# Counting edges in a graph layer: when the copies out of PSUM may start

## The chip, the cores and the metric

The kernel runs on one core of a Trainium2 chip. The metric is the device time of one execution in microseconds (us). The engines are TensorE (PE, with its weight loads shown apart as PEld), VectorE (DVE), ScalarE (ACT), GpSimd (POOL) and SyncE (SP). Each engine takes its instructions in the order in which the program lists them; what crosses from one engine to another is a wait on a semaphore.

## What is computed

Two message-passing layers on a graph of 12,500 nodes with 32 values each and 200,000 edges, sorted by destination. Cut to what matters:

```python
h = relu(layernorm(x))
# first layer: sum over edges, scaled by the degrees
hn  = h * rsqrt(max(out_deg, 1))
agg = segment_sum(hn[src], dst)
x   = x + (agg * rsqrt(max(in_deg, 1))) @ W + b
# second layer: a small network on every edge, then a mean
h   = relu(layernorm(x))
m   = mlp(concat(h[dst], h[src] - h[dst]))      # 64 -> 64 -> 128 -> 64 -> 32
x   = x + segment_sum(m, dst) / max(in_deg, 1)
```

## The kernel before

The kernel works through the edges in tiles of 128. It has three stages: out-degrees and the normalised node table (up to about 500 us of the profile), the sums of the first layer (to about 1930 us), and the second layer.

The first layer sums its messages in three ways side by side. Early chunks have their rows gathered before the degrees are known and are scaled later (`scale_rows`, tiles `look`, `mask`, `rows_scaled`). The next chunks gather rows of the finished table by indirect DMA on POOL (`gather_chunk`, `sum_rows`, PSUM tile `ps_late`). The last 491 tiles gather nothing: they are *counted* (`count_edges`), and the change is in these.

A counted tile works like this. The destinations of 128 sorted edges span at most 13 nodes (`WD`). A source node is a high part (one of 98, `PART`) and a low part (one of 128). For each edge DVE makes a one-hot row of the low part (`lo`, 128 wide) and a one-hot row of high part and destination together (`oh`, 98 x 13 wide, cut in three ranges of high parts, `THIRDS`: 33, 33 and 32 of them). The product of the two (L789) counts how many edges go from each source to each of the 13 destinations. The three ranges are 429, 429 and 416 columns; the first two go to the PSUM tile `count_two` (two banks), the third to `count_third` (one bank). ACT copies both out of PSUM into the tile `count` in SBUF (L791), as two copies of 858 and 416 columns. PSUM has one buffer of each of the two tiles, so the next tile's products wait for this tile's copies. PSUM is full: `count_two` 2 banks, `count_third`, `look`, `ps_late`, `st2`, `nu_ps` and `kept` one each.

Eight counted tiles make a group. When a group's counts are complete, `multiply` (L730) multiplies the node table with them: 98 products of 104 columns (L738, tile `st`), done in five portions of 19 or 20 during the first five tiles of the next group, then a copy (L745), a transposition (L752), another copy (L754), a placing product (L757) and an addition to the sums on DVE. In the order of PE's queue a portion stands before the tile's counts in tiles 0 to 4; the transposition and the placing product stand behind the counts of tiles 5 and 6 (`LATE`).

`count_edges` is a generator and takes one step per tile; the loop at L807 lets it run between the gathers, `sum_rows`, `scale_rows` and the node updates (`update_nodes`, tiles `nu_...`), so all of their products share PE's queue with the counts. The order is written out by hand (`manual_schedule`); the framework adds the waits.

The lines that the change touches, as they are before:

```python
ps = pp.tile([P, len(ranges), 512], F32, name=f"count_{name}")
...
    nc.tensor.matmul(
        ps[:, k, :w], lo[:, i % TPC // 2, :, i % 2], oh[:, k0 + k, :w, i % 2], start=True, stop=True)
nc.scalar.activation(
    counts[g][:, t, a:b, :].rearrange("p (k h) d -> p k (h d)", k=len(ranges)), ps[:, :, :w], AF.Copy)
```

Of the kernel before, what the change touches and what calls it, by code (L numbers as in the profile page):

```python
# [8 lines left out]
F32 = mybir.dt.float32  # L9
# [3 lines left out]
AF = mybir.ActivationFunctionType  # L13
# [3 lines left out]
P = 128  # L17
# [16 lines left out]
TPC = 4  # L34
# [50 lines left out]
def gnn_kernel(  # L85
# [20 lines left out]
    nc = tc.nc  # L106
# [133 lines left out]
    for at in pieces:  # L240
        h, a = hx[:, at, :D], xp[:, at, :]
# [44 lines left out]
    with tc.tile_pool(name="deg", bufs=3) as hp, tc.tile_pool(  # L286
        name="deg_ps", bufs=1, space=bass.MemoryType.PSUM
# [33 lines left out]
        def one_hots(name, k, width, b):  # L321

            hot = hp.tile([P, HG, width, HT], BF16, name=name)
            n = min(HG, (NT - b) // HT)
            nc.vector.tensor_tensor(  # L325
                hot[:, :n], hl[:, k, b : b + n * HT].rearrange("p (g t) -> p g t", t=HT)[:, :, None, :].to_broadcast(
                    [P, n, width, HT]), lane_g[:, None, :width, :].to_broadcast([P, n, width, HT]), op=OP.is_equal)
            return hot

        for b in batches:  # L330
            to = min(EARLY, RAW + -(-(EARLY - RAW) * (b // (HG * HT) + AHEAD_HG) // len(batches)))
            if to > gathered:
                c = slice(gathered * TPC, to * TPC)
# [5 lines left out]
            lo = one_hots("lo", 1, P, b)  # L339
            for t in range(b, min(NTR, b + HG * HT)):  # L340
                g, i = divmod(t - b, HT)
# [12 lines left out]
        for at in pieces:  # L354
            h = hx[:PART, at, :D]
# [3 lines left out]
            for k in range(3):  # L359
                t = terms[:, :, k * D : (k + 1) * D]  # L360
# [19 lines left out]
        for b in range(0, NT, P):  # L380
            n = min(P, NT - b)
# [51 lines left out]
    with tc.tile_pool(name="flag", bufs=1) as fp, tc.tile_pool(  # L433
        name="flag_ps", bufs=1, space=bass.MemoryType.PSUM
    ) as pp:
        lo = fp.tile([P, 1], F32, name="lo")
# [161 lines left out]
    with tc.tile_pool(name="e0", bufs=8) as sp, tc.tile_pool(name="nu", bufs=1) as np_, tc.tile_pool(  # L598
        name="direct", bufs=1) as dp, tc.tile_pool(name="e0_ps", bufs=1, space=bass.MemoryType.PSUM) as pp, tc.tile_pool(
        name="nu_ps", bufs=1, space=bass.MemoryType.PSUM) as np_ps:  # L600
# [113 lines left out]
        for a, b in THIRDS:  # L714
            nc.scalar.dma_start(
                table[:, a:b, :D3], tab_hn[OFF + P * a : OFF + P * b, :].rearrange("(h l) c -> l h c", l=P))
        los, onehots, counts = {}, {}, {}
        LATE = (TD - 3, TD - 2)

        def onehots_of(i):  # L720

            if i % TPC == 0:
                c = DIR * TPC + i
                los[i // TPC] = one_hots(dp, hl[:, 1, c : c + TPC], P, "lo", 3)
            onehots[i // 2] = oh = dp.tile([P, 3, KW, 2], BF16, name="oh", bufs=4)
            nc.vector.tensor_tensor(  # L726
                oh, keys[:, :, i : i + 2][:, :, None, :].to_broadcast([P, 3, KW, 2]),
                count_h[:, None, :, :].to_broadcast([P, 3, KW, 2]), op=OP.is_equal)

        def multiply(g):  # L730


            c, tiles = counts.pop(g), min(TD, ND - g * TD)
            ps = pp.tile([P, P + STEP], F32, name="st2")
            n = TD - 3
            for s in range(n):
                for h in range(PART * s // n, PART * (s + 1) // n):
                    nc.tensor.matmul(  # L738
                        ps[:, : tiles * WD], table[:, h, :], c[:, :tiles, h, :], start=(h == 0), stop=(h == PART - 1))
                if s < n - 1:  # L740
                    yield
            some = dp.tile([D3, WD * TD], F32, name="some")
            if tiles < TD:
                nc.vector.memset(some, 0.0)
            nc.scalar.activation(some[:, : tiles * WD], ps[:D3, : tiles * WD], AF.Copy)  # L745
            width = STEP * (GD - 1) + W
            place = dp.tile([WD * TD, width], F32, name="place")
            nc.vector.tensor_scalar(
                place, count_h[: WD * TD, :width, 0], pos[:, g : g + 1], None, op0=OP.is_equal)
            yield  # L750
            ps = pp.tile([P, P + STEP], F32, name="st2")
            nc.tensor.transpose(ps[: WD * TD, :D3], some, ident[:D3, :D3])  # L752
            turned = dp.tile([WD * TD, D3], F32, name="some_t")
            nc.scalar.activation(turned, ps[: WD * TD, :D3], AF.Copy)  # L754
            yield
            ps = pp.tile([P, P + STEP], F32, name="st2")
            nc.tensor.matmul(ps[:D3, :width], turned, place, start=True, stop=True)  # L757
            yield
            chunks = range(DIR + GD * g, min(NCH, DIR + GD * (g + 1)))
            sums.add(slice(0, D3), STEP * chunks[0], ps[:D3, : STEP * (len(chunks) - 1) + W], vector=True)  # L760
            added(chunks)
            yield

        def count_edges():


            before = iter(())
            onehots_of(0)
            onehots_of(2)
            for i in range(ND):  # L770
                g, t = divmod(i, TD)
                if t == 0:
                    for _ in before:
                        assert False
                    if g > 0:
                        before = multiply(g - 1)
                    counts[g] = dp.tile([P, TD, PART, WD], BF16, name="count", bufs=2)
                if i % 2 == 0 and i + 4 < ND:
                    onehots_of(i + 4)
                oh, lo = onehots[i // 2], los[i // TPC]  # L780
                if t not in LATE:
                    next(before, None)

                for ranges, name in ((THIRDS[:2], "two"), (THIRDS[2:], "third")):
                    k0, a, b = THIRDS.index(ranges[0]), ranges[0][0], ranges[-1][1]
                    ps = pp.tile([P, len(ranges), 512], F32, name=f"count_{name}")
                    w = (b - a) // len(ranges) * WD
                    for k in range(len(ranges)):
                        nc.tensor.matmul(  # L789
                            ps[:, k, :w], lo[:, i % TPC // 2, :, i % 2], oh[:, k0 + k, :w, i % 2], start=True, stop=True)  # L790
                    nc.scalar.activation(  # L791
                        counts[g][:, t, a:b, :].rearrange("p (k h) d -> p k (h d)", k=len(ranges)), ps[:, :, :w], AF.Copy)
                if t in LATE:
                    next(before, None)
                next(updating)
                yield i
            for rest in (before, multiply(NDG - 1)):
                for _ in rest:
                    next(updating)
                    yield ND  # L800

        counting = count_edges()
        LAG = 2

        QUICK = 5
        steps, stages = DIR - EARLY - 6, ND + 2 * TD
        for m in range(EARLY, DIR + LAG + 1):  # L807
# [10 lines left out]
            i = m - EARLY  # L818
# [24 lines left out]
    with tc.manual_schedule(), tc.tile_pool(name="prep", bufs=3) as prep, tc.tile_pool(name="e1", bufs=3) as ep, tc.tile_pool(name="fn", bufs=2) as fp, tc.tile_pool(  # L843
        name="p1_ps", bufs=2, space=bass.MemoryType.PSUM
# [158 lines left out]
    with tc.If(bad > 0):  # L1003
        sums0 = dram.tile([NROW, D + 1], F32, name="sums0")
        sums1 = dram.tile([NROW, D], F32, name="sums1")
        with tc.tile_pool(name="gp", bufs=1) as gp, tc.tile_pool(name="ge", bufs=1) as ge, tc.tile_pool(
            name="ge_ps", bufs=1, space=bass.MemoryType.PSUM
# [49 lines left out]
            with tc.For_i(0, NTR, 1) as i:  # L1057
                s, d, same, r = edges(i)
# [4 lines left out]
                ps = gps.tile([P, D3], F32, name="g_ps")  # L1063
# [8 lines left out]
            for q in range(NQ):  # L1072
                n = min(J, NBLK - J * q)
# [10 lines left out]
            with tc.For_i(0, NTR, 1) as i:  # L1084
                s, d, same, r = edges(i)
# [4 lines left out]
                a = ge.tile([P, HID], F32, name="g_a")  # L1090
# [17 lines left out]
                ps = gps.tile([P, D], F32, name="g_ps")  # L1108
# [7 lines left out]
            c = gp.tile([P, NBLK], F32, name="g_c")  # L1116
# [39 lines left out]
```

## Time and profile before

| What | us |
|---|---|
| Median of 3 runs (lowest, highest) | 4297.05 (4295.58, 4301.9) |
| The profiled execution, its own time | 4360.52 |
| Its span, first to last instruction | 4358.4 |
| Stretch of the first layer's sums in the profile | 498 to 1930 |
| Products of the first two ranges, L789, 982 of them | 320.5 busy |
| Copies of `count_two`, L791, 491 of them | 434.8 busy |
| Copies of `count_third`, L791, 491 of them | 252.1 busy |

How to read it: a row of the profile names the line of the kernel, the engine, the operation, what it writes and reads, shapes and number, then its busy time and the mean time of one, and last the idle time of the engine just ahead of it with what ended that idle time. In a list of waits, each row has the waiting engine and line, who ended the wait, and the sum in us, the number and the longest. In a timeline, each row has start and length in us and, in brackets, the idle time before it. The ends of products on PE are modelled, their starts are recorded. The mean granted clock of TensorE was 0.76 of full speed over the span.

### The profile page before, as it was taken

To read this page: it belongs to the slowest core of one execution; us is meant where nothing else is said; L and a number is where in the kernel's file an instruction comes from. 1 tells how busy PE (TensorE), PEld (TensorE's weight loads), DVE (VectorE), ACT (ScalarE), POOL (GpSimd) and SP (SyncE) were. 2 spreads that over 40 slices of the span, in tenths; PEclk is the share of its full clock that TensorE was granted. 3 is DMA by queue.
4 is the path that set the end of the run, shared out by engine and by line. 5 is a ranking of instruction groups with operands and counts; after the bars stand their busy time and mean duration, and the time that the engine had idled before them with its cause. 6 is when DMAs were issued, how large, how long until landed. Compare 5 with 4: busy or idle time off the path is not lost.

```text
span 4358.4 us, 54122 instructions
## 1 busy us (share of the span) xinstructions
PE 2926.1 (67%) x20860; PEld 1950.4 (45%) x20860; DVE 1822.0 (42%) x4113; ACT 1107.2 (25%) x2034; POOL 2495.7 (57%) x2655
## 2 busy tenths in 40 slices
PE   2444276777767777763667777777777777777777
PEld 2333154555555555551344444444444444444445
DVE  6555465656656566541223223222232232232233
ACT  0000254454544545430111111111111111111112
POOL 6555354545545555545566666666666666666663
PEclk9995588888888888875667777666777677677777
DMA  3110211111111111111222222222222222222221
GB/s 77 11 11 10 60 20 19 24 22 26 25 24 24 20 26 28 22 37 35 45 50 51 50 50 54 50 51 50 51 52 49 54 51 50 51 52 53 50 51 31
DMA packets 234664, 170.64 MB, mean 39 GB/s; under 512 B 156040, under 2 KB 182888, under 8 KB 234400
## 3 DMA queue, kind: packets, MB, share of 16 engines
q0 software_dynamic: 84320, 75.96, 11.6%
q1 hardware_dynamic: 131338, 85.26, 7.5%
q10 hardware_dynamic: 18742, 5.89, 0.7%
q8 instruction: 168, 2.75, 0.3%
q14 instruction: 96, 0.79, 0.1%
HBM read 153.98 MB, written 12.92 MB: 38 GB/s over the span
## 4 chain that ended last, share of the span: by engine, by line
PE 44%; another core or an unknown queue 18%; issue 14%; DVE 10%; ACT 8%; POOL 4%; DMA 1%; DVEq 0%; ACTq 0%; POOLq 0%
PE p L940 8%; ACT count L791 6%; PE p L930 6%; PE count_two L789 5%; PE st L738 5%; PE ps L958 4%; PE p L916 4%; POOL gj L211 4%; PE p L912 3%; DVE lo L325 2%; PE count_third L789 2%; PE ps_late L641 1%; DVE hi L325 1%; PE look L677 1%
## 5 line engine op out<-in xcount | busy, mean ns | idle before, releaser
L211 POOL DMA_INDIRECT gj<-tab_j,src_j x1563 | 1474.8, 944 | 912.8 <-issue 418.1
L211 POOL DMA_INDIRECT rows<-tab_hn,src_j x816 | 770.2, 944 | 755.3 <-PE ps_late L641 401.2
L940 PE MATMUL p<-w3s,h 128*128 128x64 f32 x3128 | 513.3, 322 | 158.8 <-issue 123.5
L791 ACT ACTIVATE count<-count_two 128x858 bf16<-128x858 f32 x491 | 434.8, 886 | 632.7 <-remote 270.6
L943 DVE TENSOR_TENSOR h<-p,b3n 128x512 f32<-128x512 f32 x196 | 135.2, 690 | 1052.2 <-remote 473.4
L940 PEld LDWEIGHTS p<-w3s,h 128*128 128x128 f32 x3128 | 472.3, 234 | 203.3 <-issue 159.1
L932 ACT ACTIVATE h<-p,b2s 128x1024 f32<-128x1024 f32 x196 | 217.8, 1111 | 1170.6 <-remote 453.6
L789 PE MATMUL count_two<-oh,lo 128*128 128x429 bf16 x982 | 320.5, 414 | 289.8 <-ACT count L791 219.0
L738 PE MATMUL st<-count,table 128*128 128x104 bf16 (+1 forms) x6076 | 423.2, 225 | 133.2 <-issue 82.2
L738 PEld LDWEIGHTS <-table 128*128 128x128 bf16 x6076 | 379.0, 104 | 198.1 <-issue 148.3
L930 PE MATMUL p<-h,w2s 64*128 64x512 f32 x782 | 393.2, 877 | 94.2 <-issue 80.1
L726 DVE TENSOR_TENSOR oh<-keys,kept 128x2574 bf16<-128x2574 f16 x246 | 365.5, 1487 | 60.6 <-remote 30.3
L958 PEld LDWEIGHTS ps<-hot,h 128*64 128x64 f32 x3126 | 238.2, 172 | 296.4 <-issue 174.1
L958 PE MATMUL ps<-hot,h 128*64 128x128 f32 x3126 | 272.9, 329 | 124.0 <-DVE h L943 122.3
L916 PE MATMUL p<-turned,ai 128*64 128x512 f32 x782 | 317.9, 843 | 26.7 <-issue 26.6
L789 PEld LDWEIGHTS <-lo 128*128 128x128 bf16 x1473 | 150.2, 109 | 413.6 <-issue 363.5
L342 PE MATMUL deg_ps<-hi,lo 128*128 128x98 bf16 x1563 | 183.1, 270 | 196.9 <-issue 138.3
L211 POOL DMA_INDIRECT rows_early<-tab_h,src_j x224 | 211.4, 944 | 158.0 <-DVE src_j L334 89.4
L560 DVE TENSOR_TENSOR acc<-acc,ps 64x64 f32<-64x64 f32 (+1 forms) x198 | 44.6, 225 | 594.8 <-remote 253.4
L912 PE MATMUL p<-ident,gj 128*128 128x128 f32 x784 | 199.0, 369 | 109.1 <-issue 108.5
L892 DVE TENSOR_TENSOR turned<-row,kept 128x512 f32<-128x512 f16 x391 | 249.7, 679 | 37.3 <-PE p L912 15.3
L791 ACT ACTIVATE count<-count_third 128x416 bf16<-128x416 f32 x491 | 252.1, 513 | 5.7 <-issue 1.9
(201 smaller groups left out, 2914.6 us busy)
## 6 DMA issues: line engine op xcount, KB each, us to landing
row<-rel_row SPq DMA_DIRECT2D x195, 256.0 KB
gj<-tab_j,src_j POOLq DMA_INDIRECT x1563
rows<-tab_hn,src_j POOLq DMA_INDIRECT x816
ai<-tab_i SPq DMA_DIRECT2D x195, 64.0 KB
srow<-hi_row SPq DMA_DIRECT2D x64, 98.0 KB
rows_early<-tab_h,src_j POOLq DMA_INDIRECT x224
tab_j<-nu_aij SPq DMA_DIRECT2D x23, 128.0 KB
tab_i<-nu_aij SPq DMA_DIRECT2D x23, 128.0 KB
```

The lines of the kernel that those rows point to most:

```text
L211: nc.gpsimd.indirect_dma_start(out=tile_ap, out_offset=None, in_=table, in_offset=bass.IndirectOffsetOnAxis(ap=col, axis=0))
L726: nc.vector.tensor_tensor(oh, keys[:, :, i : i + 2][:, :, None, :].to_broadcast([P, 3, KW, 2]), count_h[:, None, :, :].to_broadcast([P, 3, ...
L738: nc.tensor.matmul(ps[:, : tiles * WD], table[:, h, :], c[:, :tiles, h, :], start=(h == 0), stop=(h == PART - 1))
L789: nc.tensor.matmul(ps[:, k, :w], lo[:, i % TPC // 2, :, i % 2], oh[:, k0 + k, :w, i % 2], start=True, stop=True)
L791: nc.scalar.activation(counts[g][:, t, a:b, :].rearrange("p (k h) d -> p k (h d)", k=len(ranges)), ps[:, :, :w], AF.Copy)
L892: nc.vector.tensor_tensor(turned, v["row"][:, k], part_f.to_broadcast([P, CHUNK]), op=OP.is_equal)
L912: nc.tensor.matmul(p1[:, t, :], v["gj"][:, t].rearrange("p k c -> p (k c)"), ident, is_transpose=True, start=(t == 0), stop=False, skip_gr ...
L916: nc.tensor.matmul(p1[k * HID : (k + 1) * HID].rearrange("p t e -> p (t e)"), v["ai"][:, k], v["turned"][k], start=False, stop=True, skip_ ...
L930: nc.tensor.matmul(p2[:, k], w2s[s, :], v["h1"][s, :], start=True, stop=True)
L932: nc.scalar.activation(h2[:, :n], p2[:, :n], AF.Relu, bias=b2s)
L940: nc.tensor.matmul(p3[:, k * TPC + t, :], v["h2"][:, k, t * P : (t + 1) * P], w3s, start=True, stop=True)
L958: nc.tensor.matmul(ps[k * HID : (k + 1) * HID, o : o + W], v["h3"][:, k * TPC + t, :], v["hot"][k][:, t, :], start=(i == 0 and t == 0), st ...
```

## The change

There are three edits in `count_edges` and just above it.

First, `count_two` and `count_third` are two PSUM tiles made once, instead of being taken anew from the pool for each counted tile. Their size and number of buffers (one each) stay.

Second, the product of the third range is split in two: one of its first 8 columns and one of its other 408. Both load the same weights (`lo`). So there are four products for a tile instead of three, each with its weight load.

Third, both copies are written after all four products, and each is given a dependency on the last of them (`end`, the 408 columns). In the program that results, the copy of `count_two` waits for that product's signal instead of that of the second range, and the copy of `count_third` behind it on ACT's queue has no wait left to do. The wait of the third range for the copy of the tile before stands at the product of 8 columns. Everything else on the five engines keeps its order.

```diff
+        count_ps = {name: pp.tile([P, n, 512], F32, name=f"count_{name}") for name, n in (("two", 2), ("third", 1))}
         LATE = (TD - 3, TD - 2)
+        FIRST = 8
...
+                copies = []
                 for ranges, name in ((THIRDS[:2], "two"), (THIRDS[2:], "third")):
                     k0, a, b = THIRDS.index(ranges[0]), ranges[0][0], ranges[-1][1]
-                    ps = pp.tile([P, len(ranges), 512], F32, name=f"count_{name}")
+                    ps = count_ps[name]
                     w = (b - a) // len(ranges) * WD
                     for k in range(len(ranges)):
-                        nc.tensor.matmul(
-                            ps[:, k, :w], lo[:, i % TPC // 2, :, i % 2], oh[:, k0 + k, :w, i % 2], start=True, stop=True)
-                    nc.scalar.activation(
-                        counts[g][:, t, a:b, :].rearrange("p (k h) d -> p k (h d)", k=len(ranges)), ps[:, :, :w], AF.Copy)
+
+                        for c in (slice(0, w),) if name == "two" else (slice(0, FIRST), slice(FIRST, w)):
+                            end = nc.tensor.matmul(
+                                ps[:, k, c], lo[:, i % TPC // 2, :, i % 2], oh[:, k0 + k, c, i % 2], start=True, stop=True,
+                                skip_group_check=True)
+                    copies.append((counts[g][:, t, a:b, :].rearrange("p (k h) d -> p k (h d)", k=len(ranges)), ps[:, :, :w]))
+
+                for to, of in copies:
+                    tc.add_manual_dep(
+                        nc.scalar.activation(to, of, AF.Copy).ins, end.ins.name,
+                        mybir.DependencyInfo(mybir.DependencyClass.Sync, mybir.DependencyReason.DATA))
```

## The prediction

> **What bounds the kernel now.** I read the engines' busy time first, then the same by stretch of time, then the waits of the stretch that the change touches, then the timeline of single tiles.
>
> ```profile
> PE 2926.1 (67%) x20860; PEld 1950.4 (45%) x20860; DVE 1822.0 (42%) x4113; ACT 1107.2 (25%) x2034; POOL 2495.7 (57%) x2655
> ```
>
> No engine is full. By stretches (PE, weight loads, DVE, ACT, POOL busy us):
>
> ```profile
> 498.00:1930.00 1432.00, 1008.21 (x9940) 745.67 (x9940) 845.12 (x2317) 694.48 (x1337) 753.31 (x799) 0.83 0.16 25
> ```
>
> The 491 counting tiles all lie in this stretch (first product at 498.3 us, last at 1906.5, so 2.87 us a tile): PE 70% busy, DVE 59%, POOL 53%, ACT 48%. It is paced by waits, and these are its waits:
>
> ```profile
> POOL rows L211 <- PE ps_late L641: 399.0, 117, 7.8
> ACT count L791 <- remote: 271.1, 72, 14.7
> PE count_two L789 <- ACT count L791: 219.0, 154, 6.6
> ACT count L791 <- PE count_two L789: 140.3, 168, 6.4
> PE st L738 <- ACT count L791: 26.5, 29, 2.4
> ```
>
> POOL waits for PE, so POOL is not the bound. PE and ACT wait for each other. The timeline of three tiles without table products (L738) shows the loop on PE, then on ACT:
>
> ```profile
> 1351.69 0.54 PE L789 MATMUL count_two<-oh,lo 128*128 128x429 bf16 x2 [0.79 <-ACT count L791]
> 1352.10 0.35 PE L789 MATMUL count_third<-oh,lo 128*128 128x416 bf16 x1
> 1353.20 0.55 PE L789 MATMUL count_two<-oh,lo 128*128 128x429 bf16 x2 [0.67 <-issue]
> ```
>
> ```profile
> 1352.27 0.89 ACT L791 ACTIVATE count<-count_two 128x858 bf16<-128x858 f32 x1 [0.22 <-issue]
> 1353.05 0.51 ACT L791 ACTIVATE count<-count_third 128x416 bf16<-128x416 f32 x1
> ```
>
> The two products start at 1351.69; the first copy starts 0.58 us later, runs 0.89, and 0.05 after its end the next two products start, at 1353.20: a loop of 1.51 us. The third range's product (1352.10) runs beside the first copy, outside the loop. At the halved clock the same loop reads 1.85 us (1188.65 to 1190.49: copy 0.91 after the first product).
>
> A tile can also go like this (PE, then ACT):
>
> ```profile
> 1245.24 0.55 PE L789 MATMUL count_two<-oh,lo 128*128 128x429 bf16 x2
> 1245.62 0.35 PE L789 MATMUL count_third<-oh,lo 128*128 128x416 bf16 x1
> 1246.97 0.73 PE L738 MATMUL st<-count,table 128*128 128x104 bf16 x11
> 1248.72 0.63 PE L738 MATMUL st<-count,table 128*128 128x104 bf16 x9 [1.01 <-issue]
> ```
>
> ```profile
> 1248.81 0.89 ACT L791 ACTIVATE count<-count_two 128x858 bf16<-128x858 f32 x1 [3.28 <-remote]
> 1249.59 0.51 ACT L791 ACTIVATE count<-count_third 128x416 bf16<-128x416 f32 x1
> ```
>
> Here the first copy starts 3.57 us after its product instead of 0.58: PE's signal came late, behind a dense run of table products. Taken tile by tile from the starts in the timeline: in 155 of 491 tiles the copy starts over 1.1 us after its product (I call them late; their excess over 0.6 us is 402 us), in 336 within 1.1 us (prompt).
>
> **What the Trainium skill says.** "Perfetto Trace Analysis", section "Tensor Engine Instruction (MATMUL, LD_WEIGHTS)": a TensorE record starts at the operand prefetch and its end is estimated; the semaphore goes out only when PSUM has acknowledged the write. The trace agrees: a product's record ends 0.35 us after its start, and the copy starts 0.39 us after the last product's start, or several us later. "TensorE: Matmul & The Clock Gate", section "Part 1: The HAM clock gate": two clocks, half when the array has been idle. The trace agrees (the products of 429 columns follow each other by 0.19 or 0.36 us; 31% of tiles are at half clock). Same page, section "Wait — 56ns, not 53.3ns?": starts of products never come closer than about 25 ns, however few columns. No run here shows an 8-column product; I use it as a lower price.
>
> **The change, part by part.**
> (a) One more weight load and product a tile: 491 of each. The product has 8 columns, so the load of 128 columns before the next product sets its price. The table products, 104 columns with such a load each, follow each other by 0.052 us at full clock, 0.09 at half: I take 0.05 and 0.10, the lower end being 0.025 of the skill. The 408 columns left save 8 columns of 416, which is nothing. In tiles where PE is late rather than the copy, this lies on PE's path.
> (b) The first copy waits for the end of the third range. At full clock the last of the two products starts at +0.19, the third range at +0.39, its 408 columns at +0.44, and with 0.39 from a product's start to a copy the copy starts at +0.83 instead of +0.58: 0.25 us. At half clock: third range at +0.67, its rest at +0.77, with 0.58 the copy is at +1.35 instead of +0.91: 0.44 us.
> (c) The second copy loses its wait. It starts 0.78 us after the first, back to back, so nothing is gained; it moves with the first. On ACT's queue behind them stand the small copies of the node updates and of L745 and L754; they move by the same 0.25 to 0.44 and are waited for by DVE, which has room (59%).
> (d) The 8-column product takes over the wait for the second copy of the tile before. It stands where the third range's product stood, so PE reaches it no later; queued behind it on PE are the 408 columns and the table products, as before. In the loop both copies move together, so it waits no longer than now (0.02 to 0.03 us in a bound tile at full clock).
> (e) Fixed PSUM tiles: the order of instructions and the waits of PE, DVE, POOL and SP stay as they are apart from the added pair. Cost nothing; there was one buffer of each already.
>
> **The sum**, from the starts of each tile: how far (b) moves the copy, less the room that the next user of the buffer (or, after a group's last tile, the table products) had.
> - Tiles 4 to 6 of a group, prompt, next products bound by the copy: 63 at full clock 15.1 us, 45 at half clock 19.8 us.
> - Tiles 7 and 0 to 3, the same: 41 at full clock 4.2 us (their copies were mostly late by part of that already), 15 at half clock 6.6 us.
> - 171 prompt tiles with room: 8.3 us, and the added product of (a) where the room covers the rest, 9.4 us.
> - 155 late tiles: nothing. Third range and two products are signalled together there (in the tile above the third's product was recorded over 3 us before the copy).
> Together 63.4 us. 19.6 us of it come in tiles just before a late one; if a late signal comes a fixed time after the dense run began, they vanish in that wait. I take half, and get +53 us. Bounds: +44 (all vanish) and +79 (none vanish, and late tiles pay 0.1 us each too).
>
> The profiled execution took 4360.5 us (span 4358.4), 63 us more than the median of 4297.05. On it the sum gives 4414, on the median 4350. What PE's late signals cost without the profiler, this profile can't tell. If they were much fewer, dense table tiles would be bound by loop and PE alike: a tile of two, third and 20 table products has 0.39 + 0.19 + 1.05 = 1.62 us of PE work against a new loop of 0.83 + 0.89 + 0.05 = 1.77, about 0.15 us for up to 150 tiles more, +20.
>
> **The rivals.**
> 1. *The late signals shrink (faster).* Against the 53 us stand 402 us of late signals. In full-clock tiles, where PE had issued under 30 instructions in the 2 us before, 3 to 8% were late; with 30 to 60, about two thirds. The change pauses PE by up to 0.25 us in a tile and makes one signal of two. It decides from 53/402 = 13% fewer late microseconds; at a quarter fewer, 4297 + 53 - 100 = 4250. For it: the dependence on density. Against it: a dense table tile still issues 48 instructions in some 1.8 us, far over the 30.
> 2. *The stretch goes with the instruction count (slower still).* Tiles at full and half clock take the same mean time, 2.87 and 2.89 us, as if PE's completion rate and not its clock were the limit. 982 more instructions on the 19,880 of the stretch are 4.9%, of 1432 us 71; with some 20 us of moved copies, +90: 4387.
> 3. *Hidden (no change).* The copies move into the waits of late tiles and DVE's order decides: 4297 to 4305. Against it: 108 bound, prompt tiles lie where no table product runs.
>
> **How the numbers follow.** Forecast +53 (4350): 0.56. Rival 2: 0.16. Rival 3: 0.08. Rival 1: 0.20. A measurement of this kernel tells about 0.2% (8.6 us) from no change. Slower: 0.56 + 0.16 = 0.72; same 0.07; faster 0.21. The forecast's own range is 4340 to 4380. The range for 8 in 10 goes up to 4395 (most of rival 2) and down to 4280, which takes in rival 3 and the milder part of rival 1.
>
> **What would show it.** In the profile after: first copy 0.8 us after the first product at full clock instead of 0.58, loop of a tile without table products 1.76 instead of 1.51 (2.3 instead of 1.85 at half clock); PE's wait for the counts' copies up from 219 us; the stretch some 50 us longer, the second layer unchanged. It is wrong if the waits of ACT put down to "remote" fall by more than 60 us, if the added product costs far from 0.05 us, or if the half-clock share of 31% moves much.

## The result and the profile after

The changed kernel takes 4354.11 us (median of 4 runs, 4348.83 to 4368.51), the kernel before in the same comparison 4296.32 (4292.25 to 4301.9). The ratio is 1.0139, with a 95% interval of 1.0112 to 1.0166: 58 us slower, where +53 and 4350 were forecast.

The execution whose profile stands ahead of the prediction was 63 us over the median of its kernel; the one of the changed kernel (4348.83) is one of the runs above. So the two spans (4358.4 and 4346.7) must not be subtracted. What can be compared is single tiles. First PE, then ACT, in tiles without table products, from the timeline of the changed kernel:

```profile
800.60 0.55 PE L794 MATMUL count_two<-oh,lo 128*128 128x429 bf16 x2 [1.59 <-ACT count L801]
801.00 0.37 PE L794 MATMUL count_third<-oh,lo 128*128 128x8 bf16 x2
802.35 0.55 PE L794 MATMUL count_two<-oh,lo 128*128 128x429 bf16 x2 [0.89 <-ACT count L801]
802.75 0.37 PE L794 MATMUL count_third<-oh,lo 128*128 128x8 bf16 x2
```

```profile
801.41 0.89 ACT L801 ACTIVATE count<-count_two 128x858 bf16<-128x858 f32 x1 [0.46 <-issue]
802.19 0.51 ACT L801 ACTIVATE count<-count_third 128x416 bf16<-128x416 f32 x1
```

Products at 800.60, first copy at 801.41: 0.81 us, where it was 0.58. The copy runs 0.89 as before, and the next products start at 802.35. The loop, from one tile's first product over its copy to the next tile's first product, is 1.75 us instead of 1.51. The third range now stands inside it. ("128x8 x2" is the pair: the view merges the 8 and the 408 columns into one row.)

The waits of the same stretch as before the prediction, 498 to 1930 us (waiting engine and line, who ended the wait, us in total, times, longest):

```profile
POOL rows L211 <- PE ps_late L641: 448.3, 140, 7.8
ACT count L801 <- PE count_third L794: 271.1, 284, 6.2
PE count_two L794 <- ACT count L801: 248.6, 176, 7.2
ACT count L801 <- remote: 193.5, 53, 9.2
```

ACT's first copy now waits for the third range, and PE's wait for the copies is 249 us instead of 219. Late tiles must be counted with the limit moved by the copies' own delay (1.1 + 0.24 us at full clock, 1.1 + 0.37 at half clock): 140 instead of 155. Their excess is about 300 us instead of 402, and ACT's waits put down to "remote" (the profile does not show what ended them) are 194 us instead of 271. These are one trace each, and the trace of the kernel before is the one that is 63 us over its median. (Two expectations below speak of 124 late tiles. That number counts the tiles over 1.5 us alone; the kernel before has 137 of these.)

### The profile page after: what moved, and what is told of

It is laid out like the page before. It is cut to its first block, busy times and chain, and to the rows that moved or that the text cites. A ratio compares the mean times of both kernels' runs of the same rounds, so it can differ in the third digit from the quotient of the medians.

```text
span 4346.7 us, 55137 instructions
## 1 busy us (share of the span) xinstructions
PE 2955.4 (68%) x21351; PEld 1969.7 (45%) x21351; DVE 1823.0 (42%) x4113; ACT 1111.3 (26%) x2034; POOL 2500.6 (58%) x2655
## 4 chain that ended last, share of the span: by engine, by line
PE 44%; another core or an unknown queue 16%; issue 10%; ACT 6%; DVE 6%; POOL 1%; DMA 0%; DVEq 0%; ACTq 0%; POOLq 0%
PE p L950 9%; PE p L940 6%; ACT count L801 5%; PE ps L968 5%; PE p L926 5%; PE st L740 4%; PE count_two L794 4%; PE p L922 3%; PE count_third L794 2%; DVE hot L584 1%; DVE turned L902 1%; PE ps_late L641 1%; POOL gj L211 1%; DVE h L953 1%
## 5 line engine op out<-in xcount | busy, mean ns | idle before, releaser
L950 PE MATMUL p<-w3s,h 128*128 128x64 f32 x3128 | 499.2, 315 | 151.7 <-issue 130.4
L950 PEld LDWEIGHTS p<-w3s,h 128*128 128x128 f32 x3128 | 460.1, 228 | 197.8 <-issue 171.0
L794 PEld LDWEIGHTS <-lo 128*128 128x128 bf16 x1964 | 206.5, 111 | 509.6 <-issue 425.8
L940 PE MATMUL p<-h,w2s 64*128 64x512 f32 x782 | 379.3, 854 | 63.2 <-issue 57.4
L926 PE MATMUL p<-turned,ai 128*64 128x512 f32 x782 | 348.6, 838 | 48.4 <-issue 47.9
```

The source lines that it names most:

```text
L794: end = nc.tensor.matmul(ps[:, k, c], lo[:, i % TPC // 2, :, i % 2], oh[:, k0 + k, c, i % 2], start=True, stop=True, skip_group_check=True)
L926: nc.tensor.matmul(p1[k * HID : (k + 1) * HID].rearrange("p t e -> p (t e)"), v["ai"][:, k], v["turned"][k], start=False, stop=True, skip_ ...
L940: nc.tensor.matmul(p2[:, k], w2s[s, :], v["h1"][s, :], start=True, stop=True)
L950: nc.tensor.matmul(p3[:, k * TPC + t, :], v["h2"][:, k, t * P : (t + 1) * P], w3s, start=True, stop=True)
```

## The experiments

All twelve ran later, on four chips on which the kernel before took 3377 to 3379 us and not 4296: the same program in 21% less time. Each is compared with runs of the kernel before on its own chip, so the ratios stand; but the setting differs, and what differs is told first.

**The kernel before, once more.**

> The kernel before once more, for a trace from the same chip as the three above. Its own profiled execution was 63 us over its median; a usual one should show a span near 4295 us, and the question is which stretch is 63 us shorter and how many tiles are late. If the late tiles number well under 155 here, their number varies from run to run and the comparison of 155 with 124 says nothing of the change.

Its execution took 3379.61 us; the kernel before had a median of 3378.69 there. The expected 4295 was wrong by a fifth, and in all stages: the counts' first products start at 322 us instead of 498, the last at 1329 instead of 1907, and what follows the last table product takes 2036 us instead of 2429. The first lines of its page:

```profile
span 3377.7 us, 54122 instructions
## 1 busy us (share of the span) xinstructions
PE 2501.0 (74%) x20860; PEld 1776.6 (53%) x20860; DVE 1814.4 (54%) x4113; ACT 1115.7 (33%) x2034; POOL 2501.1 (74%) x2655
```

DVE, ACT and POOL are busy for the same time as in the first profile (1822, 1107, 2496), PE for less (2926 there), at a mean granted clock of 0.87 instead of 0.76. Late tiles: 8, not 155. Half-clock tiles: 4%, not 31%. The late signals, whose excess was 402 us in the first profile, thus do not come from the program alone, but also from where or when it ran; what makes them is not settled. Here is the wait list of its counting stretch, 322 to 1342 us:

```profile
ACT count L791 <- PE count_two L789: 258.1, 312, 7.9
POOL rows L211 <- issue: 191.1, 627, 0.3
PE count_two L789 <- ACT count L791: 84.4, 135, 5.4
```

PE waits 84 us for the copies instead of 219, "remote" is gone from the head of the list, and POOL hardly waits for PE (9 us in all): it gathers one after another, 816 times 0.945 us and some 0.3 between. On these chips the gathers run for as long as the counts do, from 339 to 1364 us.

**The change's parts, one by one.** The wait alone: in the changed kernel the split goes,

```diff
-for c in (slice(0, w),) if name == "two" else (slice(0, FIRST), slice(FIRST, w)):
+for c in (slice(0, w),):
```

> Fixed PSUM tiles and both copies waiting for the third range, whose product stays whole (416 columns, no added product). Forecast's theory: the moved first copy is nearly all of the cost, so about 45 to 58 us over the kernel before, within 15 us of the changed kernel; first copy 0.77 us after the first product at full clock. Rival 2 (instruction count): most of the cost is the added pair, so here at most +20 us. Rival 1 (late signals): the late tiles fall from 155 towards 124 here as they do in the changed kernel.

3426.85 against 3378.69 us, ratio 1.0147 (1.0131 to 1.0162): +48 us. As forecast, with the first copy at 0.79 us (median at full clock); rival 2 allowed 20. Late tiles could not fall where there were 8.

The split alone: fixed tiles, four products, and the copies where they were, each waiting for its own products.

```diff
+for c in (slice(0, w),) if name == "two" else (slice(0, FIRST), slice(FIRST, w)):
+    nc.tensor.matmul(ps[:, k, c], ..., oh[:, k0 + k, c, i % 2], start=True, stop=True, skip_group_check=True)
```

> Fixed PSUM tiles and the third range split into 8 and 408 columns, the first copy still waiting for the two products alone. Forecast's theory: the added product costs only where PE and not the copy is late, 0 to +12 us over the kernel before. Rival 2 (instruction count): +50 to +75 us, as 982 more instructions stand in the stretch. Rival 1: late tiles as many as before.

3384.46 us, ratio 1.0027 (1.0017 to 1.0037): +9 us by the ratio, +6 by the medians. Inside 0 to 12, far from 50 to 75.

The fixed tiles alone:

```diff
-ps = pp.tile([P, len(ranges), 512], F32, name=f"count_{name}")
+ps = count_ps[name]
```

> The two PSUM tiles made once, nothing else. All theories: no change, within 5 us of the kernel before, the same order and waits.

3377.89 us, ratio 0.9997 (0.9989 to 1.0006): nothing.

**The whole change in this setting.**

> The changed kernel once more, on a chip where GpSimd's gathers, and not the loop of PE and ACT, pace the kernel before. Forecast's theory: the moved copies lengthen the loop beyond the gathers' pace, +45 to +60 us, about the sum of the wait alone (+48) and the split alone (+9). Hidden (rival 3): within 9 us. Late signals shrink (rival 1): there are hardly any to shrink there, so a cost that is smaller than +40 would have another cause.

3440.36 against 3378.4 us, ratio 1.0185 (1.0171 to 1.0198): +62 us, a little over the sum of the parts (54 by the medians), and just over the expected 45 to 60. Its counting stretch, 322 to 1402 us, shows who pays:

```profile
ACT count L801 <- PE count_third L794: 338.8, 436, 5.8
POOL rows L211 <- issue: 198.4, 651, 0.3
PE count_two L794 <- ACT count L801: 110.5, 139, 5.2
POOL rows L211 <- PE ps_late L641: 85.9, 66, 5.7
```

ACT waits 81 us more, PE 26 us more (and PE is also busier: the added pair), and POOL waits 86 us for PE where it waited 9. Here is also what a tile with table products became. PE, first the kernel before, then the changed one:

```profile
638.29 0.55 PE L789 MATMUL count_two<-oh,lo 128*128 128x429 bf16 x2
638.67 0.35 PE L789 MATMUL count_third<-oh,lo 128*128 128x416 bf16 x1
638.86 1.21 PE L738 MATMUL st<-count,table 128*128 128x104 bf16 x20
639.91 0.55 PE L789 MATMUL count_two<-oh,lo 128*128 128x429 bf16 x2
```

```profile
781.11 0.55 PE L794 MATMUL count_two<-oh,lo 128*128 128x429 bf16 x2
781.50 0.37 PE L794 MATMUL count_third<-oh,lo 128*128 128x8 bf16 x2
781.71 1.21 PE L740 MATMUL st<-count,table 128*128 128x104 bf16 x20
782.90 0.55 PE L794 MATMUL count_two<-oh,lo 128*128 128x429 bf16 x2
```

Before, PE goes through without a stop, in 1.62 us. After, the 20 table products start 0.60 us after the first product instead of 0.57, and then PE stands still until the copy has ended: 1.79 us. The first copy ran from 781.97:

```profile
781.97 0.89 ACT L801 ACTIVATE count<-count_two 128x858 bf16<-128x858 f32 x1 [1.48 <-PE count_third L794]
```

Its end, 782.86, is what the next products wait for. By position in the group, from all 490 intervals between first products in the two traces: tiles 0 to 3 take 19 us more in all, tiles 4 to 6 30, tile 7 11, together 60 us (1007 to 1067). What lies ahead of the counts is as long as before, and what lies behind them 5 us shorter.

**How the cost depends on the length of the delay.** The changed kernel with the first copy waiting for the first piece of the third range, the second copy for its own product:

```diff
-                            end = nc.tensor.matmul(
+                            product = nc.tensor.matmul(
...
+                            if c.stop == FIRST:
+                                end = product
```

> As the changed kernel, but the first copy waits for the 8 columns and not for the 408 behind them; the second waits for its own product. Forecast's theory: the cost is the time by which the copy is moved, and that shrinks from 0.24 us to at most 0.05, so +5 to +15 us over the kernel before, like the split alone. A cost that belongs to waiting for another bank's product at all would give +45 or more.

3391.49 us, ratio 1.0038 (1.0024 to 1.0051): +13 us, with the copy at 0.62 us instead of 0.58 (median at full clock). The same tile in the kernel before and in this one, first product, copy and next first product:

```profile
881.00 0.55 PE L789 MATMUL count_two<-oh,lo 128*128 128x429 bf16 x2
881.58 0.89 ACT L791 ACTIVATE count<-count_two 128x858 bf16<-128x858 f32 x1
882.51 0.54 PE L789 MATMUL count_two<-oh,lo 128*128 128x429 bf16 x2 [0.68 <-ACT count L791]
```

```profile
883.54 0.54 PE L794 MATMUL count_two<-oh,lo 128*128 128x429 bf16 x2
884.16 0.89 ACT L803 ACTIVATE count<-count_two 128x858 bf16<-128x858 f32 x1 [0.17 <-PE count_third L794]
885.09 0.55 PE L794 MATMUL count_two<-oh,lo 128*128 128x429 bf16 x2 [0.69 <-ACT count L803]
```

The same with the third range cut in two halves:

> The dose between: the third range split into 208 and 208 columns, the first copy waits for the first 208. It is moved by about 0.11 us at full clock (product at +0.39, 0.30 us to its copy) where the changed kernel moves it by 0.24. Loop theory: tiles without table products pay all of it, table tiles only what exceeds the room of 0.06 us that they had, and the added pair a few us: +20 to +35 us over the kernel before. If the wait's place and not its length cost, +50 to +62 as in the changed kernel; if only long delays cost, +13 as with the 8 columns.

3404.22 against 3376.68 us, ratio 1.0075 (1.0063 to 1.0087): +28 us by the medians, with the copy at 0.69 us:

```profile
843.42 0.55 PE L794 MATMUL count_two<-oh,lo 128*128 128x429 bf16 x2 [0.88 <-ACT count L803]
844.12 0.89 ACT L803 ACTIVATE count<-count_two 128x858 bf16<-128x858 f32 x1 [0.26 <-PE count_third L794]
845.06 0.55 PE L794 MATMUL count_two<-oh,lo 128*128 128x429 bf16 x2
```

So 0.03, 0.11 and 0.23 us of delay cost 13, 28 and 62 us, the 6 to 9 us of the added product included each time. The loops of the tiles shown are 1.51 us before, then 1.55, 1.64 and, in the changed kernel, 1.75: longer by about these delays. It is the length of the delay that costs, not the fact that a copy waits for another bank's product.

**More products without the delay.** In the kernel with the split alone:

```diff
-(slice(0, FIRST), slice(FIRST, w))
+[slice(c, c + w // 4) for c in range(0, w, w // 4)]
```

> The third range in four products of 104 columns, copies as before: three added pairs a tile, 1473 of each in all. Forecast's theory: each added pair costs PE 0.025 us at full clock where PE is late, else nothing: +5 to +30 us. Rival 2 (instruction count): three times the added pair's share, 60 us or more.

3384.82 us, ratio 1.0017 (1.0008 to 1.0026): +6 us. Three added pairs cost no more than one did. The count of instructions is not the limit here; rival 2 falls, for this setting.

**Was the gathers' pace a cover?** In all three kernels below only one gather in four is made:

```diff
-                gather_chunk(rows_of[m], tab_hn[:, :], m)
+                gather(rows_of[m][:, 0, :], tab_hn[:, :], src_j[:, m * TPC : m * TPC + 1])
...
-ps[:, STEP * i : STEP * i + W], rows[:, t, :], hot[:, t // 2, :, t % 2]
+ps[:, STEP * i : STEP * i + W], rows[:, 0, :], hot[:, t // 2, :, t % 2]
```

> Takes GpSimd's cover away: of each four gathers of the middle chunks only the first is made, and its rows serve all four products (612 of 816 gathers left out; the first layer's sums of these chunks are not the reference's). Otherwise the kernel before. Loop theory: the stretch of the counts is then paced by PE and ACT, a little faster than the kernel before, 0 to 60 us, since the gathers were only just the slower. If something else paces it (DVE's one-hots), no change at all here and in the two below.

3365.43 against 3377.9 us, ratio 0.9956 (0.994 to 0.9973): -12 us. Between 340 and 1300 us POOL now stands waiting for PE,

```profile
POOL rows L211 <- PE ps_late L641: 761.2, 183, 10.7
```

so the gathers pace nothing here. PE's own waits for gathered rows fell from 20 to 4 us in the same stretch. The gathers held the kernel before back by 12 us and no more.

> The same gathers left out of the changed kernel. Loop theory: the whole price of the moved copies shows, 70 to 110 us more than the kernel before with the same gathers left out, as against +62 where the gathers covered part of it. If the 62 us have nothing to do with a cover, the same 62.

3426.81 us: +61 over the kernel before with the same gathers left out. A miss: I expected 70 to 110, and got the same 62 as with all gathers, which is what the expectation gives for no cover. The gathers cost the changed kernel about as much as the kernel before (3440.36 against 3426.81, on two chips), so they hid no part of the price.

**Shortening the loop.** One bank and one copy for each of the three ranges:

```diff
-                for ranges, name in ((THIRDS[:2], "two"), (THIRDS[2:], "third")):
+                for k, (a, b) in enumerate(THIRDS):
+                    ps = pp.tile([P, 512], F32, name=f"count_{k}")
...
+                    nc.scalar.activation(counts[g][:, t, a:b, :].rearrange("p h d -> p (h d)"), ps[:, :w], AF.Copy)
```

> Each range has a PSUM tile of one bank and a copy of its own, so that the next tile's first product waits for a copy of 429 columns and not of 858. Loop theory: PE waits less for ACT; where the loop is the bound the kernel gains (60 to 120 us); where GpSimd's gathers are, it gains nothing (within 10 us). If late signals are what paces the stretch, no gain in either place.

3361.62 against 3378.4 us, ratio 0.9949 (0.9935 to 0.9962): -17 us, faster than both kernels. That is neither what the loop as the only bound (60 to 120) nor what the gathers as the bound (at most 10) would give. Between 340 and 1300 us PE waited 12 us for the copies instead of 75, first the kernel before, then this one:

```profile
PE count_two L789 <- ACT count L791: 74.5, 126, 1.2
PE count L787 <- ACT count L789: 11.7, 41, 1.4
```

By position in the group, tiles 4 to 6, which have no table products ahead of the next tile, became 33 us shorter in all (tile 4 takes 0.99 us instead of 1.52, medians), the others 14 us longer. Tiles 2 and 3, ahead of whose next tile 20 table products stand, stayed at 1.62 and 1.63 us.

> The same gathers left out of the kernel with three tiles and three copies. Loop theory: it gains more on the kernel before with the same gathers left out than the 17 us that it gains with all gathers, 40 to 110 us. If the gathers are no cover: the same 17.

3339.59 us: -26 us against the kernel before with the same gathers left out, more than 17 but under the expected 40 to 110. With the loop shortened and most gathers out of the way the stretch from the first counted product to the last falls from 1007 us (the kernel before) only to 965. PE is busy for 861 of these 965 us and DVE for 826; what holds the stretch there was not tried.

## Why the prediction was right

**The loop.** The step that carried the forecast held. First copy at +0.83 us forecast, +0.81 measured; loop without table products 1.76 forecast, 1.75 measured; at half clock 2.3 forecast, 2.2 measured (medians of tiles 5 and 6), because the copy moved there by 0.37 us (0.91 to 1.28, medians) and not by 0.44. The table tile bound by the copy was worked out as 1.77 and is 1.79 where signals come in time. The doses show that the delay itself is what costs.

**The added pair.** Taken as 0.05 us at full clock and 0.10 at half. The start of the 408 columns follows that of the 8 by 0.025 us and 0.07 (medians). The weight load that I took for the price was hidden; the floor of about 25 ns that the Trainium skill states ("TensorE: Matmul & The Clock Gate", section "Wait — 56ns, not 53.3ns?") was the price at full clock, and this trace agrees with it. The pair alone cost 6 to 9 us where the sum had 9.4. That is luck in part: the sum charged twice the price at full clock, and for tiles of the other setting.

**The moved wait and the fixed tiles.** Nothing was forecast for the second copy's lost wait, the wait moved to the 8 columns and the fixed tiles. The fixed tiles alone are within 0.1%. The moved wait is in the split alone and the lost wait in the wait alone; neither was tried by itself. Wait alone and split alone leave some 8 us of the 62 for what the parts do together.

**The late tiles.** Here the sum was right for a reason that the runs do not fully bear out. It let 155 late tiles pay nothing and put 35 of its 63 us into tiles 4 to 6. In the first setting's two traces the intervals of tiles 4 to 6 grew by 41 us and that of tile 7 by 9, but those of tiles 0 to 3 fell by 31, so the stretch grew by 19 us where some 50 were forecast. One of the signs of being wrong came too: the waits put down to "remote" fell by 78 us, more than the 60 named (the half-clock share went from 31 to 35%). Since the trace of the kernel before was 63 us over its median, this does not show that the change gave back late signals, and it does not show the opposite. The 58 us may be the loop's 53, or a larger cost less what late signals gave back. Where hardly any signals were late, tiles 4 to 6 paid 30 of 60 us, and the table tiles, free in the forecast because so many were late, paid much of the rest. The forecast said +20 for that case, 73 in all; it was 62. That both settings give about 60 us is partly chance: in the first the tiles that could pay were fewer, but ran at half clock oftener, where the delay is 0.37 us.

**POOL as no bound.** Right in the profile that I read, where it waited 399 us for PE. In the experiments' setting its gathers ran as long as the counts, but leaving out three of four was worth 12 us and changed nothing in the price. The belief behind the experiments, that the gathers paced the kernel before, was right for 12 us only.

**The rivals.** Rival 2 (instruction count): refuted in the experiments' setting by both splits, not tried in the first. Rival 3 (hidden): refuted by the result. Rival 1 (late signals shrink): 140 late tiles against 155 and 100 us less excess point its way, with the reserve just made; the kernel was slower all the same. Whether the late signals gave back part of the cost in the first setting stays open.

## What to carry to other kernels

Where one engine fills a PSUM buffer and another empties it, and there is only one of it, write down the loop: from the first write, over the signal, the copy and its signal, to the next first write. An extra wait in it costs its length in every turn in which nothing longer runs beside it, even though no engine is busy for more than 70% of the stretch. And before a profile's waits are explained, see whether a second execution has them at all: of the 155 late tiles in this one, 8 were left where the same program ran in 3379 us.

## What the runs showed of the hardware

The same program took 4296 us on one occasion and 3379 on others; the cause stays open. DVE, ACT and POOL were busy for equally long in both, to within 1%; PE ran at half clock in 31% against 4% of the tiles, and its signals came over 1.1 us after the product in 155 tiles against 8. In the late tile that the prediction shows (its first product at 1245.24 us), PE's semaphore was not updated between 1244.42 and 1248.78 us while 43 products were recorded as started, and then it was updated four times within 0.2 us. The start of a PE record says little there of when its result could be used.
